# An expert's last tokens in half blocks of 128 rows (first feed-forward layer, one core)

## The chip, the core and the metric

The program runs on one core of a Trainium2 chip. Its metric is the device time of one execution in microseconds, the median of three runs. A core has several engines with queues of their own: PE (TensorE) multiplies matrices, PEld is the loading of its stationary operands, DVE (VectorE) and ACT (ScalarE) work elementwise, POOL (GpSimd) does small elementwise work and starts the indirect transfers (gathers and scatters), SP starts the plain transfers. The transfers themselves run on 16 DMA engines.

## The reference, cut to what matters

The model works on 2 sequences of 1024 tokens with 256 channels: a Mamba-like layer with a dense feed-forward, then a layer of experts (called the first feed-forward here), then an attention layer and a second layer of experts. The change touches only the first layer of experts:

```python
logits = -dist2 + jnp.einsum('bld,ed->ble', x, rw) + rb
topv, topi = jax.lax.top_k(logits, TOP_K)             # 4 of 16 experts for each token
w = jax.nn.softmax(topv, axis=-1)
hidden = jax.nn.gelu(jnp.einsum('bld,efd->blef', x, w1) + b1, approximate=False)   # 256 -> 1024
exp_out = jnp.einsum('blef,edf->bled', hidden, w2) + b2                            # 1024 -> 256
sel = jnp.take_along_axis(exp_out, topi[..., None], axis=2)
fused = jnp.sum(w[..., None] * sel, axis=2)
```

Here x is the pooled input of the layer, not the residual. 2048 tokens with four experts each make 8192 places. With the reference's inputs they are spread very unevenly: seven experts get 2016, 4, 46, 2048, 7, 2042 and 2029 places, the other nine get none.

## The kernel before, in words

**Blocks.** The kernel computes only the chosen experts. `slots` (line 734) sorts the places by expert, and each expert's places fill blocks of `BLK = 256` rows; the last block of an expert is padded with rows that point to rows behind the table. A block is two units of 128 rows. `slots(0)` runs when half of the tokens (the first sequence) have been routed and hands out `NB1 = 8` blocks that this half fills; `slots(1)` runs when all are routed and hands out the rest (for each expert the number of its 256-row blocks, rounded up, less those handed out already). Its results are `exi` (expert of each block, and behind them the number of blocks filled), `idx` (the token of each row, one column for each unit of 128) and `whose` (a mask that picks the expert's weight out of a gathered row).

**How many.** `slots(1)` has room for `NB = 47` blocks. `NB0 = 36` blocks are always run, in the loop over `seq`: 8 of `slots(0)`, then 28 of `slots(1)`. The other 19 of `slots(1)` stand in nested branches (`tc.If(filled > j)`) behind the loop. With the places above 35 blocks are filled, so that the 36th holds padding and no branch's body runs.

**One block** is three functions:

- `fetch` (line 912): SP reads the expert's number from `exi` and starts the transfer of its weights (`w`, 2052 KB, three buffers) and of its second bias; POOL starts a gather for each unit (`gx`, line 924).
- `turned` (line 931): PE transposes the gathered rows, four 128x128 transposes (line 935), and DVE copies the result to `gT` (line 937).
- `block` (line 940): first the fetch for the block after the next; then the first layer, eight slices `f` of 128 hidden channels, each of two matmuls (line 953; weights stationary, 256 rows moving) into one of two PSUM buffers (`mm`), which ACT reads with the Gelu into `hh` (line 954); then the transposes of the next block; then for each unit of 128 rows the second layer, eight matmuls (line 965; `hh` stationary, the 256 columns of `w2` moving), and on DVE bias and weight (lines 967 and 968); last POOL adds the unit's rows to the accumulator `acc` in DRAM (line 969). A scatter waits for the one before it, since both add to `acc`.

The matrices are f32, and the trace shows each matmul as two PE instructions, each with a weight load of its own: 32 of line 953 and 32 of line 965 for a block.

**Order.** A scheduler orders the instructions of each engine within a stretch of straight code. It interleaves the first blocks with the routing of the second sequence and with `slots(1)`; from 611 us on the blocks follow one another. The branches end such a stretch: behind the loop each engine loads `filled` into a register (line 994) and branches (line 995). A branch not taken still runs an else part in which the engine raises the semaphores that the body would have raised; on POOL this has an instruction for those of the indirect transfers (`INC_SWDGE_SEM`).

**After the blocks** SP loads `acc` back to `X` (line 1004), which waits for the semaphores of the scatters, those in the branches included, and PE transposes it for the attention layer (line 1060).

## Time and profile before

| | |
|---|---|
| median of three runs | 1664.32 us (1661.82 to 1665.44) |
| profiled execution, its own time | 1663.63 us |
| its span, first to last instruction | 1661.5 us |
| mean granted TensorE clock | 0.961 |
| busy in the span: PE, PEld, DVE, ACT, POOL | 1572.1, 1079.3, 763.8, 579.9, 339.5 us |
| blocks of the first expert layer, first and last matmul start of line 953 | 531.8 and 1074.5 us |
| the last matmul of a block ends, the next PE instruction (line 1060) starts | 1081.6 and 1093.0 us |

The span is the stretch that the trace covers; the time of an execution is some 2 us longer (1663.63 against 1661.5). In the rows of a trace the first number is a start in us from the span's start, the second a length in us, then engine, line, operation, output and inputs, and a count where several are merged. What stands in brackets is the idle time before and what ended it. A count of 32 on line 953 is 16 matmuls of the program. In a table of windows each engine's busy time is followed by its number of instructions; behind them stand the granted TensorE clock, the busy share of the DMA engines (sampling can put it a little over 1) and GB/s.

### The profile page before, as it was taken

What the parts mean: (1) busy time and instruction counts of PE and PEld (TensorE: products, weight loads), DVE (VectorE), ACT (ScalarE), POOL (GpSimd) and SP (SyncE); (2) the same over time, 40 slices, a digit from 0 to 9 for tenths busy, and PEclk for the clock granted to TensorE, in tenths of its full rate; (3) what the DMA queues carried; (4) which work ended last, traced back from release to release, by engine and by line L of the source; (5) the groups of instructions that cost most, each with busy time, mean ns of one, the idle gap of its engine ahead of it and who ended that gap; (6) DMA issues with size and microseconds to landing.
All of it is one profiled execution on the core that took longest, in us unless ns stands there. A gap on an engine that the chain in (4) does not pass through costs nothing. (4 is left out here: it accounts for less than half of the span.)

```text
span 1661.5 us, 17808 instructions
## 1 busy us (share of the span) xinstructions
PE 1572.1 (95%) x6479; PEld 1079.3 (65%) x6479; DVE 763.8 (46%) x1900; ACT 579.9 (35%) x1164; POOL 339.5 (20%) x270
## 2 busy tenths in 40 slices
PE   8989999979998999999999999969999999869997
PEld 2444466646565788888888888836555555547775
DVE  6966666672574762222222212137755776431111
ACT  4556523232422412222222222216544655212221
POOL 1100255310002113333333332210000000022221
PEclk9989899979989999999999999979999999879999
DMA  5000000030115446666666666320000100174420
GB/s 204 1 0 1 1 1 1 1 94 0 35 56 197 153 122 201 201 199 193 190 189 189 191 193 194 74 65 7 1 1 1 52 0 10 62 254 145 153 92 11
DMA packets 54303, 155.13 MB, mean 93 GB/s; under 512 B 9163, under 2 KB 41163, under 8 KB 47040
## 3 DMA queue, kind: packets, MB, share of 16 engines
q1 hardware_dynamic: 37696, 127.20, 21.6%
q0 software_dynamic: 16512, 26.73, 7.9%
q8 instruction: 52, 0.85, 0.2%
q14 instruction: 43, 0.35, 0.1%
HBM read 128.95 MB, written 25.58 MB: 93 GB/s over the span
## 5 line engine op out<-in xcount | busy, mean ns | idle before, releaser
L954 ACT ACTIVATE hh<-mm,w 128x256 f32<-128x256 f32 x288 | 136.4, 474 | 389.2 <-PE mm L953 300.9
L953 PE MATMUL mm<-gT,w 128*128 128x256 f32 x1152 | 261.8, 384 | 2.9 <-DMA w<-in_f0w 2.9
L965 PE MATMUL o<-w,hh 128*128 128x256 f32 x1152 | 255.7, 379 | 0.0
L953 PEld LDWEIGHTS mm<-gT,w 128*128 128x128 f32 x1152 | 210.1, 192 | 46.0 <-ACT hh L954 3.3
L965 PEld LDWEIGHTS o<-w,hh 128*128 128x128 f32 x1152 | 216.2, 190 | 28.0
L969 POOL DMA_INDIRECT acc<-eo,idx x72 | 114.9, 1596 | 362.2 <-DMA acc<-eo,idx 207.4
L1358 ACT ACTIVATE e<-e,nm 128x384 f32<-128x384 f32 (+7 forms) x128 | 98.6, 771 | 70.0 <-DVE nm L1351 69.3
L937 DVE COPY gT<-t 128x512 f32<-128x512 f32 x36 | 24.9, 692 | 198.6 <-PE t L935 197.5
L967 DVE TENSOR_TENSOR eo<-o,b 128x256 f32<-128x256 f32 x72 | 30.5, 425 | 177.5 <-PE o L965 171.0
L924 POOL DMA_INDIRECT gx<-prow,idx x72 | 73.1, 1015 | 187.7 <-DVE dm L626 145.7
L1351 DVE CUSTOM_DVE_ANT_0 e<-s,zneg 128x384 f32<-128x384 f32 (+7 forms) x128 | 95.4, 752 | 27.9 <-PE s L1339 22.6
L1519 PE MATMUL o<-w,hh 128*128 128x256 f32 (+1 forms) x384 | 86.1, 382 | 0.0
L1519 PEld LDWEIGHTS o<-w,hh 128*128 128x128 f32 (+1 forms) x384 | 64.9, 172 | 18.3 <-issue 2.7
L1513 ACT ACTIVATE hh<-mm,cols 128x320 f32<-128x320 f32 x64 | 33.8, 527 | 118.3 <-PE mm L1512 108.8
L1339 PE MATMUL s<-kT,qz 128*128 128x512 f32 (+3 forms) x192 | 74.0, 495 | 1.1 <-DVE nm L1351 0.9
L1512 PE MATMUL mm<-dT,w 128*128 128x320 f32 x256 | 72.6, 442 | 0.5 <-ACT dT L194 0.5
L1339 PE MATMUL s<-rT,qz 128*128 128x512 f32 (+3 forms) x192 | 70.9, 491 | 1.1 <-DVE nm L1351 1.1
L1392 PE MATMUL po<-dT,vv 128*128 128x512 f32 (+3 forms) x192 | 67.3, 503 | 0.0
L1383 PEld LDWEIGHTS t<-consts,e 128*128 128x128 f32 x288 | 36.4, 149 | 42.2 <-DVE dT L194 13.5
L1512 PEld LDWEIGHTS mm<-dT,w 128*128 128x128 f32 x256 | 48.9, 194 | 22.9 <-issue 3.7
L554 PE MATMUL mm<-h,wb 128*128 128x512 f32 x128 | 63.2, 639 | 0.0
L1383 PE MATMUL t<-consts,e 128*128 128x128 f32 x288 | 51.5, 292 | 8.0 <-DVE dT L194 4.4
(802 smaller groups left out, 2375.7 us busy)
## 6 DMA issues: line engine op xcount, KB each, us to landing
w<-in_f0w SPq DMA_DIRECT2D x36, 2052.0 KB
w<-in_f1w SPq DMA_DIRECT2D x16, 1024.0 KB
b<-in_f0b SPq DMA_DIRECT2D x36, 128.0 KB
prow<-pl SPq DMA_DIRECT2D x6, 512.0 KB
wb<-in_wb SPq DMA_DIRECT2D x1, 2560.0 KB
X<-in_x SPq DMA_DIRECT2D x2, 1024.0 KB
acc<-X SPq DMA_DIRECT2D x2, 1024.0 KB
X<-acc SPq DMA_DIRECT2D x4, 512.0 KB
```

The lines of the kernel that those rows point to most:

```text
L924: pool.indirect_dma_start(out=gx[:, h], out_offset=None, in_=prow[s], in_offset=bass.IndirectOffsetOnAxis(ap=idx[s][:, 2 * j + h : 2 * j + ...
L953: pe.matmul(p, lhsT=w1[:, k, f * P : (f + 1) * P], rhs=gT[:, k], start=k == 0, stop=k == 1)
L954: act.activation(hh[:, f], p, AF.Gelu, bias=fb[:, f : f + 1])
L965: pe.matmul(p, lhsT=hh[:, f, h * P : (h + 1) * P], rhs=w2[:, f], start=f == 0, stop=f == 7)
L969: pool.indirect_dma_start(out=acc, out_offset=bass.IndirectOffsetOnAxis(ap=idx[s][:, 2 * j + h : 2 * j + h + 1], axis=0), in_=eo, in_offse ...
L1339: pe.matmul(t[:, s0:s1], lhsT=qz[b, c, i // 2][:, 2 * hp + j, (i % 2) * P : (i % 2 + 1) * P], rhs=kT[b][:, c, s0:s1], start=True, stop=True,)
L1351: vec.tensor_tensor_reduce(out=e[:, :n], in0=ss.pop((s, u))[:, :n], in1=zneg[:, L - n :], scale=-1.0, scalar=3e38, op0=ALU.add, op1=ALU.mi ...
L1358: act.activation(e[:, :n], e[:, :n], AF.Exp, bias=nm, scale=-1.0, accum_out=r)
L1383: pe.transpose(t[:, j], e[:, (q + j) * P : (q + j + 1) * P], ident)
L1392: pe.matmul(po[:, at:], lhsT=vv[b][:, q, c, hp : hp + 2].rearrange("p h d -> p (h d)"), rhs=dT[hp, q // 4][:, q % 4, at:], start=q == 0 an ...
L1512: pe.matmul(p, lhsT=w1[:, k, f * P : (f + 1) * P], rhs=dT[:, k], start=k == 0, stop=k == 1)
L1519: pe.matmul(p[:n], lhsT=hh[:, f, s * P : s * P + n], rhs=w2[:, f], start=f == 0, stop=f == 7)
```

## The change

A block of 256 rows is kept where an expert has more than 128 places left. A rest of 1 to 128 places goes to a half block of 128 rows: one unit, so one gather, two transposes, 128 moving rows in the first layer, one pass of the second layer and one scatter. The weights are transferred as for a whole block.

- `slots(1)` has room for `NA = 39` whole blocks and for `E0 = 16` half blocks. `NA0 = 32` whole blocks (8 of `slots(0)`, 24 of `slots(1)`) and `NH0 = 4` half blocks are always run, the half blocks last. With the places above 32 whole and 3 half blocks are filled.
- The other 15 whole blocks of `slots(1)` and 12 half blocks stand in two chains of nested branches, one behind the other; each chain has a count of its own (`filled`, `halves`). In the program's text both counts are read after the eleventh block (`n == NB1 + 2`). In the order of PE's, ACT's, DVE's and POOL's instructions each load stands right ahead of its chain.
- `slots(1)` gets instructions for the second kind: nine on 128x16 and three on 128x256 elements; the table `whose` grows from 47 to 55 blocks and is filled in two pieces, and a second count is copied. `idx` and the one-hot tables keep 94 units (39 x 2 + 16).

In the order of instructions PE has eight more matmuls of blocks ahead of the first one of line 825 in `slots(1)`. Behind the branches the order is unchanged on every engine.

```diff
 BLK = 256
 NB = (B * L * TOPK - E0) // BLK + E0
-NB0 = B * L * TOPK // BLK + 4
+NA = NB - E0 // 2
+NA0, NH0 = B * L * TOPK // BLK, 4
...
         if s == 0:
...
         else:
-            vec.tensor_tensor(bl_, all_, K["m256"][:, :M].unsqueeze(1).to_broadcast(big), ALU.is_gt)
+            vec.tensor_scalar(base, all_, float(-P), None, ALU.add)
+            vec.tensor_tensor(bl_, over_e(base, big), K["m256"][:, :M].unsqueeze(1).to_broadcast(big), ALU.is_gt)
         vec.tensor_reduce(nblk, bl_, AX.X, ALU.add)
         if s == 1:
+
+            lim, nhalf, hends, delta = (c_(t, [P, E0]) for t in ("lim", "nhalf", "hends", "delta"))
+            vec.tensor_scalar(lim, nblk, float(BLK), None, ALU.mult)
+            vec.tensor_tensor(nhalf, all_, lim, ALU.is_gt)
             vec.scalar_tensor_tensor(nblk, fcut, -1.0 / BLK, nblk, ALU.mult, ALU.add)
+            vec.tensor_tensor_scan(hends, ones[:, :E0], nhalf, 0.0, ALU.mult, ALU.add)
+            vec.tensor_sub(delta, hends, nhalf)
+            vec.tensor_scalar(delta, delta, float(P), 2.0 * NA * P, ALU.mult, ALU.add)
+            vec.tensor_sub(delta, delta, lim)
...
+        if s == 1:
+            half_ = c_("half_", shape)
+            vec.tensor_tensor(half_, place, lim.unsqueeze(1).to_broadcast(shape), ALU.is_gt)
+            vec.tensor_mul(half_, half_, delta.unsqueeze(1).to_broadcast(shape))
+            vec.tensor_add(place, place, half_)
...
-                s, j = q
+                s, j, us = q
...
-                for h in range(2):
+                for h, u in enumerate(us):
                     pool.indirect_dma_start(
                         out=gx[:, h], out_offset=None, in_=prow[s],
-                        in_offset=bass.IndirectOffsetOnAxis(ap=idx[s][:, 2 * j + h : 2 * j + h + 1], axis=0),
+                        in_offset=bass.IndirectOffsetOnAxis(ap=idx[s][:, u : u + 1], axis=0),
                     )
...
+                n = len(q[2])
                 for k in range(2):
-                    for h in range(2):
+                    for h in range(n):
                         pe.transpose(t[:, k, h * P : (h + 1) * P], gx[:, h, k * P : (k + 1) * P], ident)
                 gT = tp.tile([P, 2, BLK], F32, tag="gT", name="gT")
-                vec.tensor_copy(gT, t)
+                vec.tensor_copy(gT[:, :, : n * P], t[:, :, : n * P])
...
-                        pe.matmul(p, lhsT=w1[:, k, f * P : (f + 1) * P], rhs=gT[:, k], start=k == 0, stop=k == 1)
-                    act.activation(hh[:, f], p, AF.Gelu, bias=fb[:, f : f + 1])
+                        pe.matmul(
+                            p[:, :n], lhsT=w1[:, k, f * P : (f + 1) * P], rhs=gT[:, k, :n], start=k == 0, stop=k == 1
+                        )
+                    act.activation(hh[:, f, :n], p[:, :n], AF.Gelu, bias=fb[:, f : f + 1])
                 if follow:
                     turned(follow)
-                for h in range(2):
+                for h, u in enumerate(us):
...
-            seq = [(0, j) for j in range(NB1)] + [(1, j) for j in range(NB0 - NB1)]
+            def whole(s, j):
+                return s, j, (2 * j, 2 * j + 1)
+
+            def part(j):
+                return 1, NA + j, (2 * NA + j,)
+
+            seq = [whole(0, j) for j in range(NB1)] + [whole(1, j) for j in range(NA0 - NB1)]
+            seq += [part(j) for j in range(NH0)]
...
+                if n == NB1 + 2:
+                    filled, halves = (
+                        nc.values_load(exi[1][0:1, NA + E0 + i : NA + E0 + i + 1], min_val=0, max_val=most)
+                        for i, most in enumerate((NA, E0))
+                    )
...
-            filled = nc.values_load(exi[1][0:1, NB : NB + 1], min_val=0, max_val=NB)
-            with ExitStack() as later:
-                for j in range(NB0 - NB1, NB):
-                    later.enter_context(tc.If(filled > j))
-                    fetch((1, j))
-                    turned((1, j))
-                    block((1, j), None, None)
+            for count, first, most, which in ((filled, NA0 - NB1, NA, lambda j: whole(1, j)), (halves, NH0, E0, part)):
+                with ExitStack() as later:
+                    for j in range(first, most):
+                        later.enter_context(tc.If(count > j))
+                        fetch(which(j))
+                        turned(which(j))
+                        block(which(j), None, None)
```

## The prediction

> **What bounds the kernel now.** I read the page first (its slices give the stage and its bound), then windows, the timeline of one block, the source line of the branch, and the timeline of the stage's end.
>
> PE is the bound of this stage. In the windows (us, PE, PEld, DVE, ACT, POOL busy, clock, DMA share, GB/s) PE has no idle time in a block nor in the last four blocks:
>
> ```profile
> 654.25:668.52 14.27, 14.27 (x70) 12.23 (x69) 3.19 (x10) 3.79 (x8) 4.72 (x4) 1.00 0.63 191
> 712.40:720.00 7.60, 7.60 (x39) 6.36 (x38) 0.77 (x2) 3.55 (x8) 1.62 (x1) 1.00 0.91 304
> 720.00:723.00 3.00, 3.00 (x16) 2.64 (x15) 0.87 (x3) 0.00 (x0) 1.70 (x2) 1.00 0.00 0
> 1025.00:1081.63 56.63, 56.63 (x269) 48.33 (x267) 10.01 (x27) 15.18 (x32) 14.04 (x9) 1.00 0.38 99
> ```
>
> The second and third rows show one block's weights: issued at 711.33, in transfer until 720.0, then nothing: 8.7 us from issue to landing, once a block. One block on PE, in the timeline:
>
> ```profile
> 711.05 7.09 PE L953 MATMUL mm<-gT,w 128*128 128x256 f32 x32
> ...
> 717.97 0.60 PE L935 MATMUL t<-consts,gx 128*128 128x128 f32 x4
> ...
> 718.41 7.07 PE L965 MATMUL o<-w,hh 128*128 128x256 f32 x32
> ...
> 725.32 1.03 PE L953 MATMUL mm<-gT,w 128*128 128x256 f32 x4
> ```
>
> A block lasts 725.32 - 711.05 = 14.27 us: first layer 6.92 (0.216 a row of 256 columns), transposes 0.44 (0.11 each), second layer 6.91. The nearest row to a first layer with 128 columns is a real f32 matmul with 128x128 weights and 64 columns:
>
> ```profile
> 302.42 1.90 PE L496 MATMUL py<-xdt,mt 128*128 128x64 f32 x16
> 304.25 1.12 PE L500 MATMUL pc<-S,bc 64*128 64x512 f32 x2
> ```
>
> 16 rows take 304.25 - 302.42 = 1.83 us, 0.114 a row: with so few columns the weight loads set the pace, and 0.114 is where 128 columns end too.
>
> The stage's end is a chain through POOL. First the branch's line (lengths in ns, first and last start in us), then the timeline:
>
> ```profile
> L995 POOLq EVENT_SEMAPHORE  x4: 17/43/43, 1086.7 to 1087.5; - x4
> L995 ACTq COMPARE_BRANCH  x1: 50/50/50, 1075.4 to 1075.4; - x1
> L995 ACTq EVENT_SEMAPHORE  x1: 17/17/17, 1077.9 to 1077.9; - x1
> L995 DVEq COMPARE_BRANCH  x1: 72/72/72, 1082.9 to 1082.9; - x1
> L995 POOLq COMPARE_BRANCH  x1: 57/57/57, 1084.2 to 1084.2; - x1
> L995 DVEq EVENT_SEMAPHORE  x1: 21/21/21, 1085.8 to 1085.8; - x1
> L995 POOLq INC_SWDGE_SEM  x1: 1262/1262/1262, 1087.6 to 1087.6; - x1
> ```
>
> ```profile
> 1082.29 0.35 DVE L968 TENSOR_SCALAR eo<-eo,wr 128x256 f32<-128x256 f32 x1
> 1083.84 1.55 POOL L969 DMA_INDIRECT acc<-eo,idx  x1 [2.81 <-DMA acc<-eo,idx]
> ...
> 1088.93 2.04 SPq L1004 DMA_DIRECT2D X<-acc  x4
> ```
>
> POOL's semaphore instruction ends at 1087.6 + 1.26 = 1088.9 and the load of acc starts at 1088.93: POOL's way through the untaken branch, not the data, ends last.
>
> **Part 1: four half blocks in place of four blocks.** The last four blocks take 56.63 us. With the reference's inputs 32 whole and 3 half blocks are filled, so no branch body runs, as none runs before.
>
> Second layer: 16 rows at 0.216 = 3.46 us. Transposes of the next half block: 2 at 0.11 = 0.22. First layer by PE alone: 32 rows at 0.112 (between 0.114 and the transposes' 0.11) = 3.58. PE alone: 7.26 us.
>
> But the two `mm` buffers turn too slowly for that. In the block above ACT's first Gelu starts 1.11 us after the slice's first matmul (712.16): three rows of 0.216, the fourth's length of 0.379, and 0.08. With 128 columns: 3 x 0.112 + 0.275 (line 496's median length) + 0.08 = 0.69. The Gelu of 256 columns takes 0.474; the exponential of line 1358 takes 0.504 for 256 and 0.395 for 128, so 128 columns save 0.109: 0.365. Then 0.05 to the weight load that waits, 0.11 to its matmul. A buffer is free 0.69 + 0.365 + 0.16 = 1.22 us after its slice began, while two slices are 8 x 0.112 = 0.90 us of work. So two pairs of slices take 1.22; the third 0.90 plus the first second-layer matmul, which stands there in PE's order (0.43), = 1.33; the fourth 0.90. The transposes fit into the gaps. First layer and that matmul 4.67, the other seven matmuls 3.02: 7.69 us a half block, the last without transposes 7.47.
>
> Four: 3 x 7.69 + 7.47 = 30.5. The block ahead saves two transposes, 0.22. Saved: 56.63 - 30.5 + 0.2 = **26.3 us**. Bounds: PE alone, 28.0; a first layer no faster than now (6.92, half block 10.6, four 42.2), 14.6.
>
> Weights cost nothing more: a half block of 7.7 us is shorter than the 8.7 of a transfer, but two are under way. The third half block's transfer is issued when the first starts (t), lands at t + 9 and is needed at t + 15.4; the fourth's is issued at t + 7.7, runs behind it to about t + 17.5, needed at t + 23. The cover would go with a dozen half blocks. Gathers stand further ahead in POOL's order (the last one before the scatters of the sixth-last block). Scatters under a transfer are slow (POOL's longest wait for one is 8.9 us), but each half block has only one and the last two transfers end 13 us before the end.
>
> **Part 2: a second chain of branches.** On POOL it stands between the last scatter and the load of acc. From the rows: register load 0.49 (line 994's row), compare 0.06, jump 2.4 (1084.2 and 0.06 to 1086.7), four semaphores 0.9, INC_SWDGE_SEM 1.26: 5.1 us. Against it, the last scatter no longer queues behind its twin: its rows were ready at 1082.64 and it started at 1083.84; the first scatter of that block started 0.28 after its rows, so 0.9 is saved. Net **+4.3 us**. The jump is the doubtful term: ACT (1075.45 to 1077.9) and DVE (1082.97 to 1085.8), which had nothing else to wait for, show 2.4 and 2.8. Bounds: no jump at all, +1.8; SP's jump under traffic (6.1 us) and its nine semaphores over 2.8 us in place of POOL's, +9.8. On PE, ACT and DVE the second chain costs some 3 to 4 us each and lies beside: DVE was through at 1085.9 and PE at 1082, and PE next runs at 1093.0. SP passes both while the last half blocks run.
>
> [...]
>
> **Part 3: slots(1).** Twelve instructions more, nine of 0.17 us (line 780's 128x16 form) and three of 0.42 (line 789's 128x256), and 0.7 for the wider table (880 for 752 elements at lines 835, 839, 843) and the count: 3.5 us of DVE at 565 to 580 us. PE is fed meanwhile by the blocks of slots(0): eight more of their matmuls (8 x 0.43 = 3.5 us) now stand ahead of line 825. I take +0.2; bounds -0.5 (PE waits 0.87 there today) and +3.5 if nothing covers it. The first block of slots(1) is fetched some 45 us later, so idx being later delays nothing. The counts' loads stand at the chains and stop no block.
>
> **Sum.** -26.3 + 4.3 + 0.2 = -21.8. Profiled execution 1663.63 -> 1641.8 (span 1661.5 -> 1639.7). The median is 0.7 above the profiled one: **1642.5 us**, 1.3% faster. Behind the stage the order is the same and PE starts after an idle gap as before, so the gain stays.
>
> **Rivals.**
> - The first layer does not get faster, because ACT's turn stays at a slice every 0.86 us: 14.6 saved, 1664.3 - 14.6 + 4.5 = 1654.2. For it: ACT waits for PE in every slice, and the buffers are two. Against: 0.86 is PE's own pace (4 x 0.216), not ACT's.
> - The weights set the pace: if each half block waited for a transfer, four take 4 x 8.7 = 34.8, 21.8 saved, 1647. For it: 304 GB/s at a 0.91 share leaves no room. Against: the prefetch above.
> - A long way through the second chain (+9.8): 1648.0. For it: SP's 6.1 us. Against: there is little traffic at the end (DMA share 0.46).
> - Slower: bodies in branches run. If the chip's router fills more than 32 whole or 4 half blocks, a body runs without prefetch: transfer 9, transposes and copy 1.2, then 13.8 on PE for a whole body (24 us) or 8.1 for a half (18). One whole body gives 1666.5, which is no difference; from the second body on it is slower (two half bodies 1678). Against: rests are 2016, 2042, 2029 and 2048, far from a 33rd block; two more experts would have to be chosen by a token.
>
> **How the numbers follow.** My case 0.64 (1638 to 1648: PE alone and no jump give 1638; a half block of 8.5 us with the sum's other terms 1646), slow first layer 0.14, weights 0.08, long chain 0.07, bodies 0.07. The range 1637 to 1654.5 takes in all but the bodies. A measurement here tells 0.2% (3.3 us) from no change. Faster 0.93 (the first four cases), same 0.02 and slower 0.05 (one body, two).
>
> **What would show it.** Line 953's and line 965's successors with 32 + 16 PE rows a half block, half blocks 7.3 to 8 us apart, first-layer rows near 0.112 with gaps before every third slice; ACT's Gelu on 128x128 near 0.365; two COMPARE_BRANCH and two INC_SWDGE_SEM on POOL behind the last scatter, and the load of acc right behind the second, 11.6 us after the last matmul (7.3 now). I am wrong if the last four take over 35 us, if PE waits there for weights, or if more than 32 whole blocks' Gelus appear.

## The result, and the profile after

The changed kernel takes 1636.99 us (median of 4 runs, 1635.9 to 1645.43) against 1663.07 us (4 runs, 1660.81 to 1665.44): a ratio of 0.9855, 95% interval 0.9828 to 0.9882. Timed again beside two of the experiments it took 1641.89 us (5 runs, 1633.68 to 1645.63) against 1662.57 us (9 runs): 0.9876, 0.985 to 0.9902. By the ratios the gain is 24 and 21 us; the medians themselves differ by 26.1 and 20.7 us. Predicted were 21.8 us, 1642.5 us (a ratio of 0.9869, which lies in both intervals); the first median stands at the very low end of the range (1637), the second one 0.6 us from the predicted time. In all that follows PE's end is the start of its last matmul plus the pitch of 0.216 us, as in 1081.63 for the kernel before; the row of that matmul ends 0.17 us later.

The timeline of PE in the first of the four half blocks (start, length, engine, line, operation, shapes, count):

```profile
1021.82 1.05 PE L980 MATMUL mm<-gT,w 128*128 128x128 f32 x8
1022.71 0.27 PE L961 MATMUL t<-consts,gx 128*128 128x128 f32 x1
1022.93 1.16 PE L980 MATMUL mm<-gT,w 128*128 128x128 f32 x8
1023.93 0.27 PE L961 MATMUL t<-consts,gx 128*128 128x128 f32 x1
...
1025.53 1.05 PE L980 MATMUL mm<-gT,w 128*128 128x128 f32 x8
1026.42 3.19 PE L994 MATMUL o<-w,hh 128*128 128x256 f32 x14
1029.45 1.05 PE L980 MATMUL mm<-gT,w 128*128 128x128 f32 x8
```

A half block lasts 1029.45 - 1021.82 = 7.63 us where a whole block lasted 14.27. First-layer rows come eight at a time (two slices) in 0.89 to 1.00 us, that is 0.11 to 0.125 a row; the transposes of the next half block stand between these groups of eight. The windows of the whole stretch and of PE's idle time behind it (us, PE, PEld, DVE, ACT, POOL busy, clock, DMA share, GB/s) and the group of the Gelus:

```profile
1021.82:1052.04 30.22, 30.16 (x199) 27.16 (x197) 4.82 (x12) 11.75 (x32) 7.76 (x5) 1.00 0.59 172
1052.04:1065.97 13.93, 0.18 (x1) 0.03 (x1) 1.26 (x3) 0.00 (x0) 5.19 (x6) 0.61 0.33 82
```

```profile
L983 ACT ACTIVATE hh<-mm,w 128x128 f32<-128x128 f32 x32 | 11.8, 367 | 23.3 <-PE mm L980 22.4
```

Four half blocks take 30.22 us where four blocks took 56.63. PE's gap behind them grew from 11.37 us (1081.63 to 1093.0) to 13.93. What fills the gap is POOL's way. First the timeline, then POOL's own queue on the branch's line, in short windows (lengths in ns, first and last start in us):

```profile
1053.35 1.55 POOL L998 DMA_INDIRECT acc<-eo,idx  x1 [3.38 <-DVE eo L997]
...
1061.67 2.04 SPq L1045 DMA_DIRECT2D X<-acc  x4
```

```profile
L1036 POOLq COMPARE_BRANCH  x1: 57/57/57, 1053.7 to 1053.7; - x1
L1036 POOLq EVENT_SEMAPHORE  x3: 17/42/43, 1054.2 to 1054.3; - x3
L1036 POOLq EVENT_SEMAPHORE  x1: 43/43/43, 1058.1 to 1058.1; - x1
L1036 POOLq INC_SWDGE_SEM  x1: 1097/1097/1097, 1058.2 to 1058.2; - x1
L1036 POOLq COMPARE_BRANCH  x1: 45/45/45, 1059.7 to 1059.7; - x1
L1036 POOLq EVENT_SEMAPHORE  x4: 17/43/43, 1060.1 to 1060.4; - x4
L1036 POOLq INC_SWDGE_SEM  x2: 1074/1086/1097, 1058.2 to 1060.5; - x2
```

The first chain's compare and jump take 0.5 us (1053.7 to 1054.2), the jump alone 0.4. Three semaphores come at once; the fourth starts at 1058.1, when the last scatter has landed (its packets end at 1057.7), 4.8 us after the scatter's start. Then INC_SWDGE_SEM, 1.1. The second chain begins with a register load at 1059.4, jumps within 0.4 us and ends with the second INC_SWDGE_SEM at 1061.6: the load of acc starts at 1061.67, 9.63 us after PE's end. Before, it was 7.30.

The two profiled executions differ by 27.9 us in their spans (1661.5 and 1633.6). By place: PE's first feed-forward row comes 4.0 us earlier (531.8 and 527.8), in code that the change does not touch; from there to the fourth block, where the even pitch of 14.27 begins, it is 79.4 and 80.4, so +1.1 in the stretch in which slots(1) runs; then 413.9 and 413.6 us of whole blocks, of which the missing transposes are 0.2; the last four -26.4; the gap +2.6; and behind it 568.5 and 567.6. The stage's own account is thus 1.1 - 0.3 - 26.4 + 2.6 = -23.0 us, and 4.9 us of the difference are none of the change's. That the +1.1 is the new slots(1) is not shown, since the kernel before has one profile alone; the two runs below with the same slots(1) whose timelines show this stretch have 80.5 us (the changed kernel's second) and 80.7 (one branch entry more). The granted clock from 545 to 562 us is 0.80 in the kernel before and in the changed one.

### The profile page after: what moved, and what is told of

It reads as the page before. It is cut to its first block, busy times and chain, and to the rows that moved or that the text cites. A ratio compares the mean times of both kernels' runs of the same rounds, so it can differ in the third digit from the quotient of the medians.

```text
span 1633.6 us, 17665 instructions
## 1 busy us (share of the span) xinstructions
PE 1542.9 (94%) x6407; PEld 1056.5 (65%) x6407; DVE 760.2 (47%) x1898; ACT 576.0 (35%) x1164; POOL 329.1 (20%) x262
## 5 line engine op out<-in xcount | busy, mean ns | idle before, releaser
L983 ACT ACTIVATE hh<-mm,w 128x256 f32<-128x256 f32 (+1 forms) x288 | 132.7, 462 | 370.2 <-PE mm L980 281.9
L980 PE MATMUL mm<-gT,w 128*128 128x256 f32 (+1 forms) x1152 | 251.5, 374 | 2.1 <-DMA w<-in_f0w 2.0
L994 PE MATMUL o<-w,hh 128*128 128x256 f32 x1088 | 242.6, 379 | 0.0
L980 PEld LDWEIGHTS mm<-gT,w 128*128 128x128 f32 x1152 | 203.4, 192 | 42.4 <-ACT hh L983 4.3
L994 PEld LDWEIGHTS o<-w,hh 128*128 128x128 f32 x1088 | 203.6, 190 | 26.1
L998 POOL DMA_INDIRECT acc<-eo,idx x68 | 108.4, 1594 | 346.9 <-DMA acc<-eo,idx 166.7
L963 DVE COPY gT<-t 128x512 f32<-128x512 f32 (+1 forms) x36 | 23.8, 662 | 184.2 <-PE t L961 183.2
L1392 DVE CUSTOM_DVE_ANT_0 e<-s,zneg 128x384 f32<-128x384 f32 (+7 forms) x128 | 95.5, 753 | 27.9 <-PE s L1380 22.6
L996 DVE TENSOR_TENSOR eo<-o,b 128x256 f32<-128x256 f32 x68 | 28.8, 424 | 168.9 <-PE o L994 168.9
L949 POOL DMA_INDIRECT gx<-prow,idx x68 | 68.7, 1011 | 186.6 <-DVE dm L627 145.7
```

The costliest lines, as they stand in the source:

```text
L949: pool.indirect_dma_start(out=gx[:, h], out_offset=None, in_=prow[s], in_offset=bass.IndirectOffsetOnAxis(ap=idx[s][:, u : u + 1], axis=0),)
L980: pe.matmul(p[:, :n], lhsT=w1[:, k, f * P : (f + 1) * P], rhs=gT[:, k, :n], start=k == 0, stop=k == 1)
L983: act.activation(hh[:, f, :n], p[:, :n], AF.Gelu, bias=fb[:, f : f + 1])
L994: pe.matmul(p, lhsT=hh[:, f, h * P : (h + 1) * P], rhs=w2[:, f], start=f == 0, stop=f == 7)
L998: pool.indirect_dma_start(out=acc, out_offset=bass.IndirectOffsetOnAxis(ap=idx[s][:, u : u + 1], axis=0), in_=eo, in_offset=None, compute_ ...
L1392: vec.tensor_tensor_reduce(out=e[:, :n], in0=ss.pop((s, u))[:, :n], in1=zneg[:, L - n :], scale=-1.0, scalar=3e38, op0=ALU.add, op1=ALU.mi ...
```

## The experiments

Each kernel ran once but for the last three. The single runs took 1632.15 to 1648.06 us (1730.97 with twelve half blocks). Since the code behind the stage alone varies by 8 us between runs (last section), the kernels are compared within the stage.

**First layer of the half blocks on 256 columns again.**

```diff
                 vec.tensor_copy(gT[:, :, : n * P], t[:, :, : n * P])
+                if n == 1:
+                    vec.tensor_copy(gT[:, :, P:], t[:, :, :P])
...
-                n = len(us) * P
+                n = BLK
```

> The half blocks' first layer runs on 256 columns again (the half block's 128 tokens stand twice in gT, the Gelu takes 256 columns, the second half of its result is not used); second layer, scatter and chains as in the changed kernel. Theory (the gain of the first layer comes from the columns: 32 rows at 0.11 instead of 0.216): a half block goes from 7.63 us to 6.92 + 0.22 + 3.46 = 10.60, the stretch of four from 30.2 to 3 x 10.60 + 10.38 = 42.2 us, the whole 12 us longer. Rival (a first-layer row of 128 columns is paced by ACT's turn or the weight loads, not by its columns): half block 7.6 to 8.5 us, stretch 30 to 34.

PE's timeline in it:

```profile
1026.51 7.09 PE L982 MATMUL mm<-gT,w 128*128 128x256 f32 x32
...
1033.66 3.62 PE L996 MATMUL o<-w,hh 128*128 128x256 f32 x16
1037.11 7.09 PE L982 MATMUL mm<-gT,w 128*128 128x256 f32 x32
```

A half block of 1037.11 - 1026.51 = 10.60 us, and 42.2 for the four, what the theory gives. So of the 26.4 us that the last four lost, 14.4 come from the second unit of 128 rows, which the second layer and the transposes no longer have, and 12.0 from the first layer's columns: a first-layer row of 128 columns takes 0.11 to 0.125 us in the changed kernel, one of 256 takes 0.216 (6.92 for 32), although its weights are as many. The rival "no faster first layer" falls here. Whether a short row is set by its columns or by its weight load no run tells apart: a row of 64 columns took 0.114 in the kernel before, where the weight loads were busy for 1.76 of the 1.83 us of its 16 rows, and a row of 128 columns takes 0.111 where nothing waits (three slices, below).

**Two slices in one mm buffer.**

```diff
-                    p = ps.tile([P, BLK], F32, tag="mm", name="mm")
+                    at = 0 if n == BLK else f % 2 * P
+                    if at == 0:
+                        p = ps.tile([P, BLK], F32, tag="mm", name="mm")
...
-                            p[:, :n], lhsT=w1[:, k, f * P : (f + 1) * P], rhs=gT[:, k, :n], start=k == 0, stop=k == 1
+                            p[:, at : at + n], lhsT=w1[:, k, f * P : (f + 1) * P], rhs=gT[:, k, :n], start=k == 0,
+                            stop=k == 1,
...
-                    act.activation(hh[:, f, :n], p[:, :n], AF.Gelu, bias=fb[:, f : f + 1])
+                    act.activation(hh[:, f, :n], p[:, at : at + n], AF.Gelu, bias=fb[:, f : f + 1])
```

> In a half block two slices of the first layer share one mm buffer (columns 0 to 127 and 128 to 255), so four slices are in flight instead of two. Theory (the 0.37 us that a half block takes over PE's own 7.26 are the turn of two mm buffers): half block 7.63 to 7.26 us, stretch 30.2 to 28.8. Rival (a row of 128 columns is 0.12 us by itself and the buffers cost nothing): stretch stays at 30.2.

The stretch stayed at 30.3 us, the half blocks 7.63 apart. That looks like the rival, but by the author's reading it is the edit that failed: a buffer is one tile in the program, and its second slice waits for the first one's Gelu. Which slice a row belongs to no view names, but the wait is there: after the first eight rows of the last half block the weight load waits 0.25 us for the Gelu, as long as in the changed kernel (0.25 at 1045.82):

```profile
1049.77 0.52 PEld L982 LDWEIGHTS mm<-gT,w 128*128 128x128 f32 x4 [0.25 <-ACT hh L986]
```

**Three slices under way.** Every third slice borrows a buffer of the second layer's output.

```diff
-                    p = ps.tile([P, BLK], F32, tag="mm", name="mm")
+                    p = ps.tile([P, BLK], F32, tag="o" if n < BLK and f % 3 == 2 else "mm", name="mm")
```

> In a half block every third slice of the first layer takes a buffer of the second layer's output (tag o) in place of one of the two mm buffers, so that three slices are under way instead of two. Theory (the 0.37 us that a half block takes over PE's own 7.26 are the turn of the two mm buffers: PE's weight load waits for the Gelu after the second slice): half block 7.63 to 7.26 or 7.35 us, stretch of four 30.2 to 29.1, and no gap after the first eight rows. Rival (the scatters, each of which waits for the landing of the one before, 4.5 us, or the transposes set the pace): stretch stays at 30.2. At the end the gain may be lost to the last scatter, which started only 0.3 us after its rows were ready.

```profile
1016.21 3.73 PE L980 MATMUL mm<-gT,w 128*128 128x128 f32 x32
1019.77 0.38 PE L961 MATMUL t<-consts,gx 128*128 128x128 f32 x2
1019.99 3.62 PE L994 MATMUL o<-w,hh 128*128 128x256 f32 x16
1023.45 3.73 PE L980 MATMUL mm<-gT,w 128*128 128x128 f32 x32
```

A half block of 7.24 us, the stretch 28.8 (1016.21 to 1044.97). All 32 rows of the first layer now run in one piece, 3.56 us, 0.111 a row. So the 0.37 us over PE's own time were the turn of two buffers. From the first half block's start to the load of acc it is 38.8 us against 39.85 (39.2 in the changed kernel's second run): the gain of 1.4 arrives as 1.1 at most, because the last scatter starts 1.9 us after PE's end instead of 1.3. Each scatter waits until the one before has landed: the scatters of 1039.43, 1043.88 and 1048.41 in the changed kernel's profile stand 4.45 and 4.53 us apart, the later two after a wait for the one before.

**Without the second chain.**

```diff
-                    filled, halves = (
+                    filled, = (
                         nc.values_load(exi[1][0:1, NA + E0 + i : NA + E0 + i + 1], min_val=0, max_val=most)
-                        for i, most in enumerate((NA, E0))
+                        for i, most in enumerate((NA,))
...
-            for count, first, most, which in ((filled, NA0 - NB1, NA, lambda j: whole(1, j)), (halves, NH0, E0, part)):
+            for count, first, most, which in ((filled, NA0 - NB1, NA, lambda j: whole(1, j)),):
```

> The chain of branches for half blocks and its count's load are left out (a fifth half block would not be computed; with these inputs there is none); the chain for whole blocks stays. Theory (the second pass costs what POOL's rows show: load 0.4, compare and jump 0.35, semaphores 0.4, INC_SWDGE_SEM 1.1): the load of acc starts 7.3 us after PE's last matmul of the half blocks instead of 9.6, 2.3 us earlier. The prediction's price (a jump of 2.4 us in it) would give 4.3 to 5 us earlier. Rival (the last scatter's landing ends last, and POOL's way lies beside it): no change, 9.6 us.

```profile
1049.82 0.35 DVE L997 TENSOR_SCALAR eo<-eo,wr 128x256 f32<-128x256 f32 x1
1052.76 1.55 POOL L998 DMA_INDIRECT acc<-eo,idx  x1 [4.47 <-issue]
...
1057.87 2.09 SPq L1045 DMA_DIRECT2D X<-acc  x4
```

```profile
L998 POOLq EVENT_SEMAPHORE  x1: 5540/5540/5540, 1046.5 to 1046.5; - x1
```

From PE's end (1049.14) to the load of acc it is 8.7 us, neither 7.3 nor 9.6. The reason is the first part of it: the rows of the last scatter were ready at 1050.17, yet it started at 1052.76, six us after the one before (1046.74). POOL's queue (second view) shows why: its semaphore on line 998 stands 5.54 us from 1046.5, until the scatter before has landed, which here took 5.3 us. From the scatter's start the load comes after 5.11 us, where the changed kernel needs 8.32. So the tail has two parts that have to be read apart; a table below does so for all runs.

**One branch around both chains.**

```diff
+                    if s == 1:
+                        over = c_("over", [P, 1])
+                        vec.tensor_scalar(over, ends[:, E0 - 1 : E0], float(NB1 - NA0), 0.0, ALU.add, ALU.max)
+                        vec.scalar_tensor_tensor(over, hends[:, E0 - 1 : E0], float(-NH0), over, ALU.add, ALU.max)
+                        vec.tensor_copy(exi[s][:, nb + 2 : nb + 3], over)
...
+            with ExitStack() as any_:
+                any_.enter_context(tc.If(more > 0))
+                filled, halves = (
...
+                for count, first, most, which in ((filled, NA0 - NB1, NA, lambda j: whole(1, j)), (halves, NH0, E0, part)):
```

> One branch around both chains: slots(1) works out whether any body is wanted at all (three DVE instructions more on one number), and the two counts are loaded inside it. Result and bodies as in the changed kernel. Theory (the second pass is on the path: load, compare, jump, four semaphores and INC_SWDGE_SEM, 2.35 us): the load of acc starts 5.1 us after the last scatter's start, as with one chain, instead of 8.3. Rival (a jump over both chains is far, and takes 2.4 us or more on POOL): up to 2 us of it is lost if it isn't hidden under the scatter's landing, 5 to 7 us. Second rival (the landing ends last whatever the chains do): 7 to 8 us.

```profile
1055.83 1.55 POOL L1003 DMA_INDIRECT acc<-eo,idx  x1 [2.97 <-DVE eo L1002]
...
1061.77 2.50 SPq L1053 DMA_DIRECT2D X<-acc  x4
```

5.94 us from the scatter's start to the load of acc, 2.4 less than with two chains (5.1 were expected; the landing took 4.6 here and 3.9 in the run with one chain); from the first half block's start PE's idle time ends after 41.5 us (1024.30 to 1065.82) instead of 44.15. The far jump over both chains did take its 3.0 us on POOL, from 1056.2 to 1059.2, but under the scatter's landing, which ended at 1060.5. So the second pass itself was on the path, and the landing alone does not set the end.

**A second chain that is far.** The first try raised only the loop's end:

```diff
-            for count, first, most, which in ((filled, NA0 - NB1, NA, lambda j: whole(1, j)), (halves, NH0, E0, part)):
+            for count, first, most, which in ((filled, NA0 - NB1, NA, lambda j: whole(1, j)), (halves, NH0, 2 * E0 - NH0, lambda j: part(min(j, E0 - 1)))):
```

> The chain for half blocks gets 24 bodies in place of 12 (the twelve more stand under counts that are never reached; none runs), so that its jump on POOL goes over 48 DMA issues, more than before's 44, in place of 24. Theory (a jump is short, 0.3 to 0.5 us, while its target is near, and 2.4 us when it is far): the second pass takes 2 us more, the load of acc starts 11.7 us after PE's last matmul, and DVE's second jump goes from 0.3 to 2.8. Rival (the second jump is short because it follows another one, or a jump's length does not depend on its distance): 9.6 us as in the changed kernel, DVE's second jump 0.3.

This run must be read otherwise than its expectation says. The count is declared to be at most 16, so the bodies beyond were dropped from the program: it is the changed kernel with one branch entry more on POOL, and not a test of distance. (Its figure for before was wrong as well: the chain of before has 19 bodies and 76 DMA issues, not 44, and the changed kernel's first chain 15 bodies and 60.) As a repeat it warns: the load of acc did start 11.8 us after PE's end, as the theory had it, but not by a jump, which took 0.4; the last scatter's landing took 6.8 us in this run instead of 4.75. The total agreed and its cause did not.

The second try raises the bound too, and has 56 bodies:

```diff
-                        for i, most in enumerate((NA, E0))
+                        for i, most in enumerate((NA, 60))
...
-            for count, first, most, which in ((filled, NA0 - NB1, NA, lambda j: whole(1, j)), (halves, NH0, E0, part)):
+            for count, first, most, which in ((filled, NA0 - NB1, NA, lambda j: whole(1, j)), (halves, NH0, 60, lambda j: part(min(j, E0 - 1)))):
```

> The second chain gets 56 bodies in place of 12 (the 44 more stand under counts that are never reached, none runs; this time the bound on the count is raised too, so that the program really has them): on POOL its jump goes over some 280 instructions in place of 60, where before's one goes over 114 and the changed kernel's first over 90. Theory (a jump is short while its target is near, long when it is far): POOL's second jump goes from 0.35 us to 2.4, DVE's from 0.3 to 2.8, the load of acc starts 2 us later after the first chain's INC_SWDGE_SEM (5.5 us after its start instead of 3.5). Rival (the second jump is short because it follows another one, whatever its distance): 0.35 on POOL, 0.3 on DVE, 3.5 us.

POOL's queue from the end of the first chain on:

```profile
L1036 POOLq INC_SWDGE_SEM  x1: 1097/1097/1097, 1057.6 to 1057.6; - x1
L1036 POOLq COMPARE_BRANCH  x1: 45/45/45, 1059.2 to 1059.2; - x1
L1036 POOLq EVENT_SEMAPHORE  x4: 17/42/43, 1061.7 to 1061.9; - x4
L1036 POOLq INC_SWDGE_SEM  x1: 1077/1077/1077, 1062.0 to 1062.0; - x1
```

The jump takes 2.45 us (1059.2 and 0.045 to 1061.7) instead of 0.35, and the load of acc starts at 1063.22, 5.6 us after the first INC_SWDGE_SEM; expected were 5.5, by the rival 3.5. DVE's second jump goes from 0.2 to 4.3. So with the target farther away the same jump became dear: over some 280 entries of POOL's program it costs 2.45, before's jump over 114 costs 2.4 (from its branch's rows), and the changed kernel's over 90 and 60 about 0.4 each.

Distance is not all of it, though. On ACT the changed kernel's first jump, over 15 whole blocks, takes 0.4 us, and its second, over only 12 half blocks, 2.0:

```profile
L1036 ACTq COMPARE_BRANCH  x2: 45/48/50, 1050.7 to 1053.9; - x2
L1036 ACTq EVENT_SEMAPHORE  x2: 17/17/17, 1051.1 to 1055.9; - x2
```

And in the kernel with twelve half blocks always (below) POOL's first jump, over the same 15 whole blocks as in the changed kernel, takes 3.9 us:

```profile
L1036 POOLq EVENT_SEMAPHORE  x4: 17/43/43, 1146.9 to 1147.2; - x4
L1036 POOLq COMPARE_BRANCH  x1: 57/57/57, 1143.0 to 1143.0; - x1
```

So the jump over the same bodies took 0.4 us in one kernel and 3.9 in the other, and the number of bodies alone does not set it. What does, these runs do not show.

**A half block in a branch's body.**

```diff
-NA0, NH0 = B * L * TOPK // BLK, 4
+NA0, NH0 = B * L * TOPK // BLK, 2
```

> Only two half blocks always (NH0 = 2): the third filled half block runs in a branch's body, the fourth, empty one, not at all. Theory of the prediction (a body runs without prefetch: transfer of the weights 9, transposes and copy 1.2, PE 8.1 = 18 us): PE's stretch 15.0 us, then a gap of some 15 us, a body of 7.6 us, and the load of acc 3 us later than in the changed kernel, counted from the start of the first half block (40 us in that kernel). Rival (SP, which passes the branches ahead of time, starts the transfer while PE is in the half blocks, so that only POOL's gather, behind the first chain, is late): a gap of 8 to 10 us, the load of acc 4 to 6 us earlier than by the theory, about 35 us after that start. Counted in the whole: +3 or -3 us.

SP's wait for the body's weights, and the body on POOL and PE:

```profile
L942 SPq EVENT_SEMAPHORE  x1: 21380/21380/21380, 1021.0 to 1021.0; - x1
```

```profile
1042.47 0.34 SPq L942 DMA_DIRECT2D w<-in_f0w  x1
...
1048.72 1.02 POOL L949 DMA_INDIRECT gx<-prow,idx  x1 [6.58 <-issue]
...
1053.39 3.77 PE L980 MATMUL mm<-gT,w 128*128 128x128 f32 x16 [0.56 <-issue]
...
1069.12 2.38 SPq L1045 DMA_DIRECT2D X<-acc  x4
```

SP does reach the branch early, as the rival says, but then waits 21.4 us before it may issue the transfer, until 1042.4, 3.1 us after PE's end; for what, no view names. The weights land 9.0 us after their issue, at 1051.5, and POOL's gather ends PE's wait just behind, at 1052.1. From the first half block's start to the load of acc it is 44.8 us, 5.0 more than in the changed kernel (expected 3, rival -5). One body costs 15.3 + 5.0 = 20.2 us where the prediction had 18: from PE's last matmul of the half blocks (1039.28) to the body's first layer it is 14.1 us (10.2 expected); that layer's first 16 rows take 3.56 us, 0.22 a row where it was 0.11 to 0.125 in the half blocks, so the body's PE time is 9.1 us instead of 8.1; in return the tail behind it is 3.0 shorter, 6.6 us.

**Twelve half blocks always.** The same line with 12 in place of 4.

> Twelve half blocks always in place of four (NH0 = 12; the eight more are padding with weights of the last expert), in the changed kernel. The prediction said that the weights' cover would go with a dozen. Theory (weights, 8.7 us from issue to landing against 7.63 of PE): lateness of 1.07 us from about the ninth half block on, stretch 91.3 + 3.2 = 94.5 us. Rival (transfers one behind the other need only the 7.6 us in which they move): 91.3. Second rival (scatters: each waits for the landing of the one before, 8.4 to 10 us under a weight transfer, more than a half block): the half blocks go to 8.5 us or more from the fourth on, stretch 98 to 110.

POOL's timeline and one row of DVE in the middle of the stretch, and what PE waited for in all of it:

```profile
1074.13 1.58 POOL L998 DMA_INDIRECT acc<-eo,idx  x1 [8.40 <-DVE wr L991]
1076.01 1.01 POOL L949 DMA_INDIRECT gx<-prow,idx  x1 [0.30 <-issue]
...
1084.43 0.17 DVE L990 TENSOR_TENSOR mine<-gx,whose 128x16 f32<-128x16 f32 x1 [10.04 <-DMA gx<-prow,idx]
...
1085.65 1.58 POOL L998 DMA_INDIRECT acc<-eo,idx  x1 [8.62 <-DVE wr L991]
```

```profile
PE mm L980 <- DVE gT L963: 20.4, 7, 5.0
```

119.0 us (1020.14 to 1139.15), more than the theory and both rivals have. From 1062.83 to 1108.50 the scatters stand 11.3 to 11.5 us apart, one for each half block, and PE waits for gT seven times, 20.4 us in all. POOL paces them, as the second rival says, but not by its wait alone. Each gather stands behind a scatter in POOL's order. In the stretch shown DVE waits 10.0 us until 1084.4 for the gathered rows, 8.4 us after the gather's start (1076.01), and the rows of the next scatter, gT and POOL's next issue (1085.65) come behind that wait. The changed kernel's profile shows one scatter held up beside a weight transfer: of the scatter of 1021.95, with weights issued at 1022.10, no packet moves before 1026 and the last ones after 1031, while all packets of the one before (1017.40) had moved by 1021.4. Whether the same holds the gathers up here is not shown. Only the last four, for which no gather is left, stand 7.6 to 7.7 us apart.

**The two improvements together, and three half blocks.** The first kernel combines the borrowed buffer and the single branch; the second has NH0 = 3 besides. The unedited changed kernel was timed beside them.

> The changed kernel once more, unedited, timed beside the two that follow on the same chip, for its own spread and its own tail. Expected: 24 us below the kernel before, as recorded; half blocks 7.63 us apart again. Of the tail: if the 4.75 us of the last scatter's landing belong to the program, they come again within 0.3; if they are a matter of the single run, 3.7 to 6.8.

> Three slices under way and one branch around both chains, together. Theory (both are on the path to the load of acc, and the chain behind it does not give them back): 1.1 us by the slices and 2.4 us by the branch, 3.5 us less than the changed kernel timed beside it, about 0.2%; from the first half block's start to the load of acc 36.4 us instead of 39.85. Rival (the rest of the program, whose granted clock depends on PE's gap, takes it back): no difference within 1 us.

> As the one before, and only three half blocks always (NH0 = 3), the fourth in a branch: with these inputs three are filled, so the empty one falls away and no body runs. Theory: 7.25 us less than the kernel with four, 10.8 us less than the changed kernel, 35 us less than the kernel before (ratio 0.979). Rival (an empty half block lies beside the scatters, which are late and pace the end, 4.5 us each): 3 to 5 us less than with four.

The changed kernel: 1641.89 us, half blocks 7.63 apart; its last scatter landed after 4.2 us where it had been 4.8, so that is a matter of the single run. Both edits: 1639.82 (5 runs, 1637.66 to 1644.94), ratio to before 0.9858 (0.9833 to 0.9883); its interval overlaps the changed kernel's, so no difference is shown in the whole time. With three half blocks: 1627.59 (5 runs, 1621.75 to 1627.89), ratio 0.9784 (0.9761 to 0.9807), the fastest here, 14.3 us below the changed kernel by medians (10.8 expected). It computes everything, but a fourth filled half block would then pay a body.

In the stage itself, from the first half block's start to the load of acc: 39.2 us in the changed kernel's new run (39.85 in its first), 38.2 with both edits, 29.6 with three half blocks. So both edits bring 1.1 to 1.7 of the 3.5 us expected, and the empty half block 8.5 (7.25 expected; the rival's 3 to 5 falls). Of the 14.3 us, then, 9.6 to 10.2 lie in the stage; the rest is in code that the edits do not touch, and that the whole time came out at the expected ratio is in part luck. The end of the kernel with both edits shows what took the rest:

```profile
1051.44 3.62 PE L999 MATMUL o<-w,hh 128*128 128x256 f32 x16
1054.19 1.55 POOL L1003 DMA_INDIRECT acc<-eo,idx  x1 [2.91 <-DMA acc<-eo,idx]
1058.90 1.74 POOL L1003 DMA_INDIRECT acc<-eo,idx  x1 [3.15 <-issue]
...
1064.29 2.04 SPq L1053 DMA_DIRECT2D X<-acc  x4
```

PE ends at 1054.9, but the second-last scatter starts only at 1054.19 and the last one 4.7 us behind it. The scatters are the chain that ends last in this run: those that were held up before (the one of 1049.73 starts 5.6 us behind the one of 1044.13) are caught up at 4.5 to 4.7 us each, and a shorter half block would not have helped. With the same half blocks and two chains (three slices, above) the last scatter started only 1.9 us after PE's end, so how far they fall behind differs from run to run.

**The tail of the runs in which no body runs.** (a) is from PE's last matmul of the stage to the last scatter's start, (b) from there to the load of acc, of which "landed" is the time to POOL's last semaphore of the first pass (all in us, from the timelines and POOL's queue):

| kernel | passes | (a) | landed | (b) |
|---|---|---|---|---|
| before | 1, far | 2.2 | 3.7 | 5.1 |
| one chain | 1 | 3.6 | 3.9 | 5.1 |
| one branch around both | 1, far | 1.3 | 4.6 | 5.9 |
| both edits | 1, far | 4.0 | 4.1 | 5.4 |
| both edits, three half blocks | 1, far | 3.0 | 3.9 | 5.2 |
| changed, first run | 2 | 1.3 | 4.8 | 8.3 |
| changed, second run | 2 | 1.3 | 4.2 | 7.7 |
| changed, one entry more | 2 | 1.5 | 6.8 | 10.3 |
| two slices in a buffer | 2 | 2.6 | 4.7 | 8.2 |
| three slices | 2 | 1.9 | 4.6 | 8.2 |
| first layer on 256 columns | 2 | 1.3 | 5.2 | 8.8 |
| 56 bodies | 2, second far | 3.8 | 5.2 | 10.9 |
| twelve half blocks | 2, first slow | 3.4 | 4.6 | 7.2 |

With one pass (b) is 5.1 to 5.9, far or not; with two near ones 7.7 to 8.8, but for the run whose landing took 6.8. The slow first jumps are over before the landing, at 1059.2 against 1060.5 with one branch and at 1146.9 against 1147.2 with twelve half blocks, and from the landing to the load of acc it is 1.3 us with one branch and 1.2 with one chain. The second pass itself (behind the first INC_SWDGE_SEM) is 2.35 us in the changed kernel. The landing varies by 3.1 us (3.7 to 6.8) between runs of nearly the same program.

## Why the prediction was right, point by point

- **Part 1, four half blocks: right, and by its own steps.** Half block 7.69 predicted, 7.63 measured; the last 7.47 and 7.33 (1044.70 to 1052.04); four 30.5 and 30.2; Gelu 0.365 and 0.367; saved 26.3 and 26.4 + 0.2. The row of 64 columns (0.114) was a good price for 128 columns: 0.111 when nothing waits. The turn of two buffers was 0.43 by the prediction and 0.37 to 0.39 by the runs: three buffers take it away. The low bound, four at 42.4 (42.2 if the last one's missing transposes are left out), is what 256 columns gave (42.2).
- **Weights: right for four.** PE had 30.16 us of work in 30.22. The reserve ("a dozen half blocks") was wrong: with twelve, POOL's scatters and gathers bind, at 11.3 to 11.5 us from scatter to scatter, before the weights' own pace (8.7 from issue to landing) would. From how many on they bind no run shows.
- **Part 2, the second chain: right in place and kind, too dear.** Predicted net +4.3 on the way from PE's end to the load of acc, measured +2.3 in the profiled run (9.63 against 7.30; 1.7 in the second run, 4.5 in the one with an entry more). The pass cost 2.35 and not 5.1. The step that failed is "jump 2.4", taken from before's POOL rows: the second jump took 0.4. The run with 56 bodies, in which its target is farther, gives the 2.4 back. The four semaphores took 0.3 and not 0.9, since before's 0.9 held the wait for the scatter's landing, which the second pass does not have again. (The terms as listed add up to 4.2, not 4.3.) The 0.9 for the last scatter's queueing was saved as predicted (2.2 to 1.3). What the sum did not have is the landing: 4.8 against 3.7, which took back 1.1 of it, and which varies between runs.
- **Part 3, slots(1): within its bounds, its size not shown.** +0.2 predicted; from the stage's first row to the even pitch it is 79.4 us in the one profile of the kernel before, and 80.4 to 80.7 in three profiles with the new slots(1): +1.1 to +1.3, within the bounds (-0.5 to +3.5).
- **Rivals.** Slow first layer: refuted by the 256-column run, which is 12.0 us longer in the stretch. Weights pace: not with four. Long chain: not as it stood; the 56 bodies show that it can become long (a jump of 2.45 us, and 10.9 us from the last scatter's start to the load of acc). Bodies: none ran, 32 whole and 3 half blocks were filled; the price of one half body was 20.2 us and not 18.
- **The sum.** -21.8 predicted; the stage's own account gives -23.0 in the profiled run: PE's gap grew by 2.6 instead of 4.3 (a near jump, against a landing 1.1 longer), the stretch of slots(1) took 0.9 more, and the blocks saved 0.4 more. That the total is off by 1.2 us only is in part luck, since a pass 2.7 us too dear stands against a landing and a stretch that were too cheap. The medians are 26.1 and 20.7 us apart. What is left between them and the account lies in code that the change does not touch; the runs of the changed kernel between 1642 and 1646 us have a mean granted clock of 0.956 or 0.957, its fastest 0.961, and the kernel before 0.959 to 0.963. Whether the change itself makes the lower clock more frequent is not shown. Five runs of the one kernel lie 12 us apart, so the prediction's "0.2% (3.3 us)" is less than a single run can tell.

## What to carry to other kernels

Do not copy a jump's price from another place: over a chain that is not taken POOL's jump cost 0.4 us in one place and 2.4 to 3.9 in another, and a farther target is only one of the reasons. Where the last scatter's landing covered it, it cost nothing here (3.0 us until 1059.2, under a landing until 1060.5); what stayed was the rest of the pass, 2.35 us for the second chain with its register load, near jump, semaphores and an INC_SWDGE_SEM of 1.1 us, so put one branch around several chains (2.4 us of the stage here). When a stage's matmuls get shorter, ask next for the queue with the fixed price per block, here POOL's scatters and gathers: two scatters fit into a whole block's 14.3 us, but with twelve half blocks one scatter and one gather took 11.3 us or more and did not fit into 7.6. And where an experiment's total agrees, look at its parts all the same: one run here met its number by another cause.

## What the runs showed of the hardware that was not expected

The rest of the program behind the stage is the same code in all these kernels, and takes 567.4 to 568.6 us in some runs and 570.3 to 575.3 in others. The windows from 180 to 240 and 400 to 480 us behind PE's restart, first of the changed kernel, then of the one with a single branch, show PE's granted clock (the third column from the end):

```profile
1245.97:1305.97 60.00, 58.12 (x242) 34.46 (x241) 35.54 (x129) 32.28 (x88) 1.04 (x1) 1.00 0.11 36
...
1465.97:1545.97 80.00, 80.00 (x338) 58.02 (x337) 12.63 (x28) 17.34 (x35) 19.46 (x20) 1.00 0.40 139
```

```profile
1245.82:1305.82 60.00, 58.68 (x233) 35.08 (x232) 32.95 (x115) 29.11 (x81) 1.04 (x1) 0.95 0.11 36
...
1465.82:1545.82 80.00, 79.19 (x318) 56.88 (x318) 10.78 (x24) 18.70 (x37) 22.08 (x23) 0.95 0.46 149
```

From the restart to the end PE is busy for 531.5 us in the one and 538.9 us in the other. With 7.4 us between two runs in code that is the same a whole time can't tell 3 us, and the stage has to be compared in itself. That this clock follows PE's gap, as a rival above has it, no run shows: at 1.00 the gap was 13.93 us in the changed kernel and 11.37 in the kernel before (1273 to 1333), at 0.95 it was 11.28 with the single branch.

The granted clock also falls to half behind the stage: in the gap of the changed kernel it is 0.76 from 1054 to 1056 and 0.50 from 1056 on, and it stays at 0.50 until some nine us after PE restarts at 1065.97 (0.50 from 1072 to 1074, 0.62 from 1074 to 1076, then 1.00). In the run with a half block in a branch's body, the first 16 rows of that body took 0.22 us each, against 0.111 where nothing waits.

The last scatter lands 3.7 to 6.8 us after its start. While it lands, the DMA queues that the profile names instruction move packets too: 4 in the kernel before, with a landing of 3.7 us, and 7 in the changed kernel, with one of 4.8. Whether they stand in the scatter's way no run shows. The last scatter started 2.6 us after its rows were ready in the run with one chain and 3.0 in the one with both edits: it is the landing of the one before it for which POOL waits, 5.54 us on line 998 with one chain. Why that landing is 5.3 us long there stays open too.
